# Trainium2, a fused attention and quantized-feed-forward layer: the first chunk's projections by seven products, and the squared norms' products behind a unit's scores

## The chip, the cores and the metric

The kernel runs on one core of a Trainium2 chip. The metric is the device time of one execution in microseconds. A profile of one further execution was taken; its rows are named by engine: PE is TensorE's products, PEld its weight loads, DVE is VectorE, ACT is ScalarE, POOL is GpSimd, SP is SyncE, which issues most loads and stores.

## The reference

For x of 8 x 1024 rows of 512 floats the reference computes (cut to what matters):

```python
x = x + layernorm(attention(layernorm(x), Wq, bq, Wk, bk, Wv, bv, Wo, bo))
x = x + layernorm(ffn(layernorm(x), weight))

# attention, 16 heads of 32
scores = einsum('bhid,bhjd->bhij', Q, K) / sqrt(32)
scores = where(causal_mask, -inf, scores) + where(causal_mask, 0, -(i - j))
out = einsum('bhij,bhjd->bhid', softmax(scores), V) @ Wo.T + bo

# ffn
xh = x @ hadamard(512)
xq = 4-bit rounding of xh, one scale a row
wq = ternary rounding of weight, one scale a row
return xq @ wq.T
```

## The kernel before, in words

The 8192 rows are 16 chunks of 512 rows (two chunks a sequence), and each chunk is four row tiles of 128. The penalty that grows with distance lets a query look at its own and the preceding keys of a band only, so a chunk needs its own keys and the last tile of the chunk before it. A chunk's work is cut into eight units: two halves of 256 queries by four groups of four heads. All of it is one program in an order written out by hand: every engine takes its instructions in the order in which the code names them, and semaphores tell it when an input is ready or a buffer free. No scheduler moves anything.

The steady loop (lines 819 to 916) runs over the chunks and, in each, over pairs of units. While chunk c's units are computed, the loop also does three other things: it projects chunk c+1 (class `Projections`), it normalises tiles of chunk c+2 (`norm_in`), and it runs the rest of the layer for finished row tiles (`rest`, two at a time). One pair of units is: scores of the first unit; values of the unit before; two of the products of the projection; parts of norm and rest; scores of the second unit; values of the first unit; more products. `scores` (line 559) writes the one PSUM tile `s` and ScalarE's Exp (line 585) reads it out with a bias; GpSimd masks (line 596) and adds the two key halves (line 610); `values` (line 616) multiplies with v (line 626) and with ones for the sums (line 637); VectorE divides (lines 655 to 660).

The projection of a chunk from the second on is made by seven products instead of eight, for each of q, k and v: the 512x512 product is cut into 2x2 blocks, sums of blocks of the weights and of xnT are made first, seven block products are computed in `ORDER` (line 379), and their sums are the result. `Weight.combine` and `Weight.replace` (lines 359 and 370) make the weights' sums once, on GpSimd; `replace` overwrites blocks of the weight. `Projections.combine` (line 387) makes the sums of xnT, `product` (line 405) issues four 128x256 products into one PSUM bank (line 417), and `drain` (line 422) adds the bank to the results: ScalarE for the first, VectorE for the others. Three PSUM banks (`Banks`, line 292) take turns for everything that is not scores or values; `bank(n)` names the one that the next tile takes.

The Exp's bias needs a bound on the scores. For the next chunk, `square` squares q and later k on ScalarE, `bound` (line 477) issues four small products that sum the squares by head (`norms_of`, line 333, 128x32 shapes in TensorE), `largest` reduces them on VectorE, and `multiply`, `spread_max` and `shift` (lines 490, 522 and 505) turn them into the bias. In each chunk of the loop, `bound` is called twice, in the pairs u = 4 (q) and u = 6 (k), ahead of the second unit's scores.

The first chunk cannot be projected under another chunk's units, so the start (lines 690 to 788) does it alone: the loads, the normalisation of four tiles and their transposes, then `project_v` four times, k four times and q four times (`project_qk`), each a 512x512 block column by four full 128x512 products (line 153) drained by ScalarE. Between them stand the norm tiles of chunk 1 (`ahead_norms`), the weights' sums on GpSimd and the steps of `prepare` (line 1170). `prepare` rounds the feed-forward weight to three values (a reduction for the scales, line 1175; thresholds, lines 1185 and 1187; transposes, line 1198), makes the row of scales (line 1213) and adds Wo times bv to the output bias: bv is spread over 128 columns and multiplied with Wo in four products (line 1221). Lastly `first.multiply` and `first.shift` make chunk 0's bias.

Of the kernel before, what the change touches and what calls it, by code (L numbers as in the profile page):

```python
# [40 lines left out]
def sandwich_kernel(  # L41
# [262 lines left out]
    def band():  # L304
# [71 lines left out]
        class Projections:  # L376
# [10 lines left out]
            def combine(self, which, engine=nc.gpsimd):  # L387

                x = self.ch.xnT
                b11, b12 = x[:, :HB, :HW], x[:, :HB, HW:]  # L390
                b21, b22 = x[:, HB:, :HW], x[:, HB:, HW:]
                if which == 0:
                    t = big.tile([P, KD, HB, HW], F32, tag="T", name=f"T_{self.ch.n}", bufs=1)
                    self.t = t
                    engine.tensor_tensor(t[:, 0], b12, b11, ALU.subtract)
                    engine.tensor_tensor(t[:, 1], b22, t[:, 0], ALU.subtract)
                    self.parts = {1: b11, 2: b21, 3: b22, 5: t[:, 0], 6: t[:, 1]}
                elif which == 1:
                    nc.gpsimd.tensor_tensor(self.t[:, 2], b22, b12, ALU.subtract)
                    self.parts[7] = self.t[:, 2]  # L400
                else:
                    nc.gpsimd.tensor_tensor(self.t[:, 3], self.t[:, 1], b21, ALU.subtract)
                    self.parts[4] = self.t[:, 3]
# [100 lines left out]

            def shift(self):


                ch = self.ch
                shift = small.tile([P, 1], F32, tag="shift", name=f"shift_{ch.n}")
                nc.gpsimd.tensor_tensor(shift, spread_max(self.diag, ch.n), half1, ALU.pow)  # L510
                nc.gpsimd.tensor_scalar(shift, shift, -SLACK, -0.5, ALU.mult, ALU.add)
                nc.gpsimd.tensor_scalar(shift, shift, ROUND, None, ALU.add)
                nc.gpsimd.tensor_scalar(shift, shift, ROUND, None, ALU.subtract)
                ch.bias = small.tile([P, 2, 2], F32, tag="bias", name=f"bias_{ch.n}")
                nc.gpsimd.tensor_scalar(ch.bias, decay_cols, shift, None, ALU.add)

# [158 lines left out]
        def start_rest(ch, t):  # L675
# [11 lines left out]
            )  # L687


        x0 = big.tile([P, TPC, D], F32, tag="pr", name="x0")  # L690
# [14 lines left out]
        ch.xnT = big.tile([P, KD, CT], F32, tag="xnT", name=f"xnT_{ch.n}")  # L705
        ch.kT = big.tile([P, KD, CT], F32, tag="kT", name=f"kT_{ch.n}")
        ch.qT = big.tile([P, KD, CT], F32, tag="qT", name=f"qT_{ch.n}")
        ch.v = big.tile([P, TPC, D], F32, tag="v", name=f"v_{ch.n}")
        made = []
# [17 lines left out]

        def squares_of_q(o0, o1):
            nc.scalar.activation(sqq[:, o0:o1, :], ch.qT[:, o0:o1, :], AF.Square)

# [7 lines left out]
        transposed(0)  # L738
        first = Projections(ch, None)
        prep = prepare(pools, wf_sb)  # L740
        ahead_steps = {0: "01", 1: "02", 2: "0", 3: "132", 4: "1", 5: "23", 6: "2", 7: "3", 8: "3"}
        for i in range(3 * KD):
            if i % 2 or not i:
                for t in ahead_steps.get(i, ""):
                    next(ahead_norms[int(t)])
            which, o = divmod(i, KD)
            if which == 0:
                project_v(pools, wv_sb, ch.v, ch.xnT, o, ch.n)
            elif which == 1:
                project_qk(pools, "k", wk_sb, bk_sb, ch.kT, ch.xnT, o, ch.n)  # L750
            else:
                project_qk(pools, "q", wq_sb, bq_sb, ch.qT, ch.xnT, o, ch.n)
            if i == 0:
                transposed(1)
                normalised(3)
                transposed(2)
            elif i == 1:
                transposed(3)
            elif i == KD - 1:
                prepare_q(wq_sb)  # L760
                nc.gpsimd.tensor_tensor(bqk_step[:, 0], bq_sb[:, HB:], bq_sb[:, :HB], ALU.subtract)
                nc.gpsimd.tensor_tensor(bqk_step[:, 1], bk_sb[:, HB:], bk_sb[:, :HB], ALU.subtract)
                weights[2].combine()
                weights[2].replace()
                weights[1].combine()
            elif i == 2 * KD - 1:
                weights[0].combine()
                weights[1].replace()
                sqk = squares(ch, "k", ch.kT)
                sqq = row.tile([P, KD, CT], BF16, tag="sq", name=f"sqq_{ch.n}", bufs=1)  # L770
            elif i == 2 * KD:
                ch.mk = largest_of(ch, "k", norms_of(ch, "k", sqk))
            elif i == 2 * KD + 2:
                squares_of_q(0, HB)
            if i and i % 2 == 0:
                for t in ahead_steps.get(i, ""):
                    next(ahead_norms[int(t)])
            if i in (KD, 6, 2 * KD):
                next(prep)
        squares_of_q(HB, KD)  # L780
        next(prep)
        next(prep)
        ch.mq = largest_of(ch, "q", norms_of(ch, "q", [sqq[:, o, :] for o in range(KD)]))
        first.multiply()
        next(prep)
        first.shift()
        next(prep)
        weights[0].replace(nc.vector)

# [20 lines left out]
        rests_due = ahead(start_rest(ch, t) for ch in chunks for t in range(TPC))  # L810
        def bank(at):
            pools.ps_m.named = at


# [4 lines left out]
        for at, ch in enumerate(chunks[:-1]):  # L819
# [7 lines left out]
            for u in range(0, 2 * NG, 2):  # L827

                new = Unit(ch, before, u)
                new.scores()  # L830
# [13 lines left out]
                proj.drain()  # L844
                norm = next(norms_due)
                steps(norm, 1)
                bank(two)
# [12 lines left out]
                steps(rest_b, 1)  # L860
                steps(rest_a, 1)
                if u >= 4:
                    bank(held)
                    proj.bound()

                new = Unit(ch, before, u + 1)
                new.scores()
                unit.values()
                if u >= 4:
                    held, one, two = one, two, held  # L870
                bank(held)
                proj.product()
                steps(rest_b, 1)
                if u >= 4:
# [295 lines left out]
    def prepare(pools, wf_sb):  # L1170
# [3 lines left out]
        ws = const.tile([P, KD], F32, name="wscale")  # L1174
        nc.vector.tensor_reduce(ws, w, AX.X, ALU.add, apply_absolute_value=True)
        nc.vector.tensor_scalar(ws, ws, 1.0 / D, SCALE_MIN, ALU.mult, ALU.max)
# [3 lines left out]
        nc.vector.tensor_scalar(lo, ws, -0.5, None, ALU.mult)  # L1180
        diag = row.tile([P, KD, P], F32, tag="u", name="wdiag", bufs=1)

        def ternary(k):
            below = row.tile([P, D], F32, tag="y", name=f"below_{k}", bufs=1)
            nc.vector.tensor_scalar(below, w[:, k, :], lo[:, k : k + 1], None, ALU.is_lt)
            tern = row.tile([P, D], BF16, tag=("qi", "qiT")[k % 2], name=f"tern_{k}", bufs=1)
            nc.vector.scalar_tensor_tensor(
                tern, w[:, k, :], hi[:, k : k + 1], below, ALU.is_gt, ALU.subtract
            )
            nc.vector.tensor_scalar(  # L1190
                diag[:, k, :], ident, ws[:, k : k + 1], 1.0 / QPOS, ALU.mult, ALU.mult
            )
            return tern

        def transposed(k, tern):
            pt = pools.ps_m.tile([P, KD, P], BF16, tag="pm", name=f"ternT_ps_{k}")
            for i in range(KD):
                nc.tensor.transpose(pt[:, i, :], tern[:, i * P : (i + 1) * P], ident_bf)
            nc.vector.tensor_copy(ternT[:, :, k * P : (k + 1) * P], pt)

        terns = [ternary(k) for k in range(2)]
        yield
        for k in range(2):
            transposed(k, terns[k])
        terns += [ternary(k) for k in range(2, KD)]
        yield
        nc.vector.tensor_copy(had0_sb, had_sb)
        nc.vector.memset(had0_sb[:, 0:1], 0.0)
        bvw = row.tile([P, KD, P], F32, tag="wT", name="bvw", bufs=1)
        nc.vector.tensor_copy(bvw, bvT_sb.unsqueeze(2).to_broadcast([P, KD, P]))  # L1210
        yield
        pr = pools.ps_m.tile([P, D], F32, tag="pm", name="wscale_ps")
        nc.tensor.matmul(pr, ones, diag.rearrange("p k q -> p (k q)"), start=True, stop=True)
        nc.vector.tensor_copy(wscale_row, pr)
        yield
        for k in range(2, KD):
            transposed(k, terns[k])
        yield
        ps = pools.ps_m.tile([P, D], F32, tag="pm", name="bo2_ps")
        for k in range(KD):  # L1220
            nc.tensor.matmul(
                ps, bvw[:, k, :], wo_sb[:, k, :], start=(k == 0), stop=(k == KD - 1)
            )
            if k == KD // 2 - 1:
                yield
        nc.vector.tensor_tensor(bo2, ps, bo2, ALU.add)
        yield
# [51 lines left out]
```

## Time and profile before

| | |
|---|---|
| median of 3 runs | 1396.66 us (1395.66 to 1398.48) |
| the profiled execution | 1396.07 us, its span 1394.3 us |
| granted TensorE clock | 0.995 of full speed |
| busy share of the span | PE 98%, PEld 69%, DVE 73%, ACT 49%, POOL 64% |
| span of the start, to the first scores | 61.94 us |

The span reaches from the first to the last instruction; the execution's own time is 1.8 us longer. In a line of the timeline the first figure is the start in us from the span's start and the second the duration; the number behind x is the count of records (an f32 product leaves two records), and a bracket names idle time just before and what ended it. In a line of the waits the figures are the sum in us, how many times, and the longest.

### The profile page before, as it was taken

The numbers are of one execution on the slowest core, as the hardware profiler recorded it, in microseconds if no ns is written. First come the engines' busy times: TensorE is split into PE (matmuls) and PEld (weight loads), VectorE is DVE, ScalarE is ACT, GpSimd is POOL, SyncE is SP. The second block draws the span as 40 slices with busy tenths as digits, with TensorE's granted clock in tenths as the row PEclk, the third lists the DMA queues.
The fourth block names the chain that finished last, engine by engine and source line by source line (L and its number), as shares of the span: only waits on it lengthen the run. The fifth ranks groups of instructions, "written<-read, shape, count | busy, mean of one in ns | idle before, by whom it ended". The sixth has DMA issues, their size and how long they took to land.

```text
span 1394.3 us, 35003 instructions
## 1 busy us (share of the span) xinstructions
PE 1363.4 (98%) x14504; PEld 967.5 (69%) x14504; DVE 1015.7 (73%) x2167; ACT 681.2 (49%) x1176; POOL 892.0 (64%) x1280
## 2 busy tenths in 40 slices
PE   9999999999999999999999999999999999999895
PEld 5577777777767777767776777777776777766553
DVE  5467777777777776777777777877777777777675
ACT  3345454545445455554545545445544545535442
POOL 4565758576576767658676676757757666665434
PEclk9999999999999999999999999999999999999998
DMA  6010011011011011011011011011101101000010
GB/s 228 8 47 24 24 47 46 24 47 47 24 47 47 24 47 47 32 39 47 30 41 46 25 47 47 28 43 47 40 31 47 47 24 47 25 23 32 32 39 33
DMA packets 31750, 58.23 MB, mean 42 GB/s; under 512 B 4064, under 2 KB 4448, under 8 KB 31584
## 3 DMA queue, kind: packets, MB, share of 16 engines
q1 hardware_dynamic: 30720, 54.87, 11.4%
q8 instruction: 116, 1.90, 0.5%
q10 hardware_dynamic: 864, 1.05, 0.2%
q14 instruction: 50, 0.41, 0.1%
HBM read 39.13 MB, written 16.78 MB: 40 GB/s over the span
## 4 chain that ended last, share of the span: by engine, by line


## 5 line engine op out<-in xcount | busy, mean ns | idle before, releaser
L585 ACT ACTIVATE pr<-s,bias 128x512 f32<-128x512 f32 (+1 forms) x512 | 295.3, 660 | 138.5 <-PE s L571 138.5
L610 POOL TENSOR_TENSOR both<-pr 128x1024 f32<-128x1024 f32 (+1 forms) x120 | 250.5, 2088 | 5.2
L153 PE MATMUL o_ps<-wo_sb,oT 128*128 128x512 f32 x512 | 236.1, 604 | 0.6
L596 POOL TENSOR_SCALAR_AFFINE_SELECT pr<-pr 128x1024 f32<-128x1024 f32 x128 | 150.0, 1172 | 108.2 <-ACT pr L585 103.8
L153 PEld LDWEIGHTS o_ps<-wo_sb,oT 128*128 128x128 f32 x512 | 93.2, 192 | 95.2 <-issue 92.5
L187 DVE TENSOR_TENSOR y<-o_ps,bo 128x512 f32<-128x512 f32 x64 | 44.2, 691 | 150.5 <-PE o_ps L153 150.5
L626 PE MATMUL av<-pr,v 128*32 128x128 f32 (+1 forms) x2816 | 130.7, 316 | 1.8 <-DVE oT L660 1.8
L571 PE MATMUL s<-qT,kT 32*64 32x192 f32 (+2 forms) x5632 | 119.9, 285 | 1.5 <-ACT pr L585 1.5
L571 PEld LDWEIGHTS s<-qT,kT 32*64 32x64 f32 x5632 | 99.8, 131 | 31.0 <-issue 21.6
L141 ACT ACTIVATE xn<-xc,nmr,rstd_n 128x512 f32<-128x512 f32 x60 | 48.8, 814 | 140.0 <-POOL nmr L139 140.0
L119 POOL TENSOR_SCALAR rstd_a<-mv_a 128x1 f32<-128x1 f32 x64 | 13.9, 217 | 142.7 <-DVE mv_a L127 141.5
L226 ACT ACTIVATE wT<-h_ps 128x512 f32<-128x512 f32 x64 | 38.2, 597 | 133.8 <-PE h_ps L218 133.8
L626 PEld LDWEIGHTS av<-pr,v 128*32 128x32 f32 x2816 | 74.9, 110 | 35.4 <-issue 1.8
L212 ACT COPY wT<-wT_ps 128x512 f32<-128x512 f32 x64 | 37.5, 585 | 123.4 <-PE wT_ps L210 123.4
L238 DVE TENSOR_REDUCE sc<-h_ps 128x1 f32<-128x512 f32 x64 | 44.1, 689 | 63.8 <-ACT wT L226 63.8
L119 POOL TENSOR_SCALAR rstd_c<-mv_c 128x1 f32<-128x1 f32 x64 | 14.7, 229 | 116.1 <-DVE mv_c L127 116.0
L285 POOL TENSOR_TENSOR y<-y,x 128x512 f32<-128x512 f32 x63 | 80.6, 1279 | 1.3 <-ACT y L284 1.3
L637 PE MATMUL av<-both,ones 128*32 128x256 f32 x960 | 74.2, 381 | 0.5 <-POOL both L614 0.5
L218 PEld LDWEIGHTS h_ps<-had_sb,wT 128*128 128x128 f32 x512 | 66.8, 192 | 6.2 <-ACT wT L212 3.3
L218 PE MATMUL h_ps<-had_sb,wT 128*128 128x128 f32 x512 | 68.1, 276 | 2.1 <-ACT wT L212 2.1
L153 PE MATMUL f_ps<-ternT,qiT 128*128 128x512 bf16 x256 | 66.2, 382 | 2.4 <-ACT qiT L257 2.4
L146 ACT COPY xnT<-xnT_ps 128x512 f32<-128x512 f32 x60 | 35.2, 586 | 56.8 <-PE xnT_ps L145 56.8
(213 smaller groups left out, 3100.7 us busy)
## 6 DMA issues: line engine op xcount, KB each, us to landing
xr<-in_x SPq DMA_DIRECT2D x64, 256.0 KB, 2.9
out<-y SPq DMA_DIRECT2D x63, 256.0 KB, 2.0
xc<-in_x SPq DMA_DIRECT2D x60, 256.0 KB, 2.7
wv_sb<-in_wvT ACTq DMA_DIRECT2D x4, 256.0 KB, 5.1
x<-in_x SPq DMA_DIRECT2D x4, 256.0 KB, 4.9
wk_sb<-in_wkT SPq DMA_DIRECT2D x1, 1024.0 KB, 6.7
wq_sb<-in_wqT SPq DMA_DIRECT2D x1, 1024.0 KB, 9.0
wf_sb<-in_wf SPq DMA_DIRECT2D x1, 1024.0 KB, 10.7
```

Of the source, the lines that this page charges most:

```text
L141: nc.scalar.activation(xn, xc, AF.Identity, bias=nmr, scale=r)
L153: nc.tensor.matmul(ps, lhs(k), rhs(k), start=(k == 0), stop=(k == KD - 1))
L187: nc.vector.tensor_tensor(y, ps, bo2, ALU.add)
L218: nc.tensor.matmul(xh[:, k * P : (k + 1) * P], wT[:, k, :], had_sb if k else had0_sb, start=True, stop=True,)
L238: nc.vector.tensor_reduce(sc, xh, AX.X, ALU.max, apply_absolute_value=True)
L285: nc.gpsimd.tensor_tensor(y2, y2, x1, ALU.add)
L571: nc.tensor.matmul(s[half * hp : (half + 1) * hp, hh, column[which] + c0 : column[which] + c1], kc.kT[hsl, g, k0 : k0 + hp], ch.qT[hsl, g, ...
L585: nc.scalar.activation(pr[:, :, r0:, own, cols], s5[:, :, r0:, own, cols], AF.Exp, bias=ch.bias[:, own, h : h + 1],)
L596: nc.gpsimd.affine_select(out=own, in_=own, compare_op=ALU.is_ge, fill=0.0, base=0, pattern=[[0, HPG], [0, 2], [1, P]], channel_multiplier=-1,
L610: engine.tensor_tensor(self.both[:, :, r0:], pr[:, :, r0:, 0, :], pr[:, :, r0:, 1, :], ALU.add)
L626: nc.tensor.matmul(av[hh * HD : (hh + 1) * HD, 0, qc : qc + w], kc.v[:, at, h * HD : (h + 1) * HD], pr[:, hh, sc : sc + w], start=(at_part ...
L637: nc.tensor.matmul(av[hh * HD : (hh + 1) * HD, 1, :], ones[:, :HD], self.both[:, hh].rearrange("p r c -> p (r c)") if own is None else sel ...
```

## The change

There are three parts. First, chunk 0's k and q are made by the seven products (`first.product` and `first.drain`, with `first.done` set to 7 for k and to 0 for q), and v stays as it was. For this the sums of wk stand on GpSimd during the projection of v, those of wq behind them, those of wv after q; the sums of chunk 0's xnT are made on VectorE; the steps of `prepare`, of the norm tiles and of the squares are spread anew between the products, with named banks at the end. The scales' reduction becomes four passes on ScalarE with a sum. Second, the bias is made of weighted rows: GpSimd multiplies the rows of Wo by bv and adds the four blocks, and one product with ones sums over the partitions. Third, in the steady loop `proj.bound()` is issued behind the second unit's scores instead of ahead of them. With these go smaller moves: the shift's last four operations of chunk 0 run on VectorE, the first norm tile of the loop starts ahead of the first scores, and for the first two pairs of chunk 0 the values of the first unit stand behind one product.

```diff
-    nc.gpsimd.tensor_tensor(self.t[:, 2], b22, b12, ALU.subtract)
+    engine.tensor_tensor(self.t[:, 2], b22, b12, ALU.subtract)
...
-            def shift(self):
+            def shift(self, engine=nc.gpsimd):
                 nc.gpsimd.tensor_tensor(shift, spread_max(self.diag, ch.n), half1, ALU.pow)
-                nc.gpsimd.tensor_scalar(shift, shift, -SLACK, -0.5, ALU.mult, ALU.add)
+                engine.tensor_scalar(shift, shift, -SLACK, -0.5, ALU.mult, ALU.add)
...
-        for i in range(3 * KD):
-            which, o = divmod(i, KD)
-            if which == 0:
-                project_v(pools, wv_sb, ch.v, ch.xnT, o, ch.n)
-            elif which == 1:
-                project_qk(pools, "k", wk_sb, bk_sb, ch.kT, ch.xnT, o, ch.n)
-            else:
-                project_qk(pools, "q", wq_sb, bq_sb, ch.qT, ch.xnT, o, ch.n)
...
+        for t in range(TPC):
+            if t == 0:
+                go(0, 1)
+            elif t == 1:
+                go(0, 2)
+            elif t == 3:
+                go(1, 3, 2)
+            project_v(pools, wv_sb, ch.v, ch.xnT, t, ch.n)
+            if t == 0:
+                transposed(1)
+                normalised(3)
+                transposed(2)
+                weights[1].combine()
+            elif t == 1:
+                transposed(3)
+                prepare_q(wq_sb)
+                weights[1].replace()
...
+            elif t == 2:
+                go(0)
+                for kind in range(3):
+                    first.combine(kind, nc.vector)
+            else:
+                weights[0].combine()
+                weights[0].replace()
+                next(prep)
+        kinds = len(Projections.ORDER)
+        first.done = kinds
+        for i in range(kinds):
+            first.product()
+            first.drain()
+            if i in (0, 2, 4):
+                go((1, 2, 3)[i // 2])
+            elif i in (1, 3):
+                go((2, 3)[i // 2])
+            next(prep)
+        sqk = squares(ch, "k", ch.kT)
+        first.done = 0
+        for i in range(kinds):
+            first.product()
+            first.drain()
+            if i == 1:
                 ch.mk = largest_of(ch, "k", norms_of(ch, "k", sqk))
...
+        weights[2].combine()
+        weights[2].replace()
...
         ch.mq = largest_of(ch, "q", norms_of(ch, "q", [sqq[:, o, :] for o in range(KD)]))
         first.multiply()
+        bank(0)
         next(prep)
-        first.shift()
+        bank(2)
+        go(3)
+        bank(1)
+        first.shift(nc.vector)
         next(prep)
...
+                if at == u == 0:
+                    norm = next(norms_due)
+                    steps(norm, 1)
                 new = Unit(ch, before, u)
                 new.scores()
...
-                if u >= 4:
-                    bank(held)
-                    proj.bound()
 
                 new = Unit(ch, before, u + 1)
                 new.scores()
-                unit.values()
+                if u >= 4:
+                    bank(held)
+                    proj.bound()
+                late = at == 0 and u < NG
+                if not late:
+                    unit.values()
...
                 proj.product()
+                if late:
+                    unit.values()
...
-        nc.vector.tensor_reduce(ws, w, AX.X, ALU.add, apply_absolute_value=True)
+        for k in range(KD):
+            nc.scalar.activation(below, w[:, k, :], AF.Abs, accum_out=ws[:, k : k + 1])
...
+        bvw = row.tile([P, D], F32, tag="wT", name="bvw", bufs=1)
+        nc.gpsimd.tensor_scalar(bvw, wo_sb[:, 0, :], bvT_sb[:, 0:1], None, ALU.mult)
+        for k in range(1, KD):
+            more = row.tile([P, D], F32, tag="w", name=f"bvw_{k}", bufs=1)
+            nc.gpsimd.tensor_scalar(more, wo_sb[:, k, :], bvT_sb[:, k : k + 1], None, ALU.mult)
+            nc.gpsimd.tensor_tensor(bvw, bvw, more, ALU.add)
...
-        for k in range(KD):
-            nc.tensor.matmul(
-                ps, bvw[:, k, :], wo_sb[:, k, :], start=(k == 0), stop=(k == KD - 1)
-            )
+        nc.tensor.matmul(ps, ones, bvw, start=True, stop=True)
         nc.vector.tensor_tensor(bo2, ps, bo2, ALU.add)
```

## The prediction

> **What bounds the kernel now.** I read the page first, then TensorE's waits, then the timelines of the start and of one stretch of the steady loop. The chain of waits answers with no piece here, so the bound is read from TensorE itself.
>
> ```profile
> PE 1363.4 (98%) x14504; PEld 967.5 (69%) x14504; DVE 1015.7 (73%) x2167; ACT 681.2 (49%) x1176; POOL 892.0 (64%) x1280
> ```
>
> Busy ends of PE are modelled, so 98% alone proves little. The waits of PE between 160 and 1290 us do: three, 0.6 us in all, in 1130 us.
>
> ```profile
> PE wT_ps L210 <- DVE u_v L453: 0.4, 2, 0.2
> PE wT_ps L210 <- DVE w L202: 0.2, 1, 0.2
> ```
>
> So PE's queue sets the end from the first projection to the tail, and a microsecond taken from it early shifts everything after. PE's timeline of the start (start, duration, engine, line, tiles, count, idle before) prices what is replaced:
>
> ```profile
> 24.87 3.60 PE L153 MATMUL k_ps<-xnT,wk_sb 128*128 128x512 f32 x8
> 28.31 0.60 PE L145 MATMUL xnT_ps<-ident,xn 128*128 128x128 f32 x4
> ...
> 55.73 1.02 PE L1213 MATMUL wscale_ps<-wdiag,ones 128*128 128x512 f32 x2
> 56.59 0.61 PE L1198 MATMUL ternT_ps<-ident_bf,tern 128*128 128x128 bf16 x8
> 57.54 0.61 PE L333 MATMUL nq<-sqq,head_rows 128*32 128x512 bf16 x4 [0.34 <-DVE wscale_row L1214]
> 58.08 1.98 PE L1221 MATMUL bo_ps<-wo_sb,bvw 128*128 128x512 f32 x4
> 59.90 0.38 PE L525 MATMUL m_ps<-diag,ones 128*128 128x128 f32 x2
> 60.12 1.88 PE L1221 MATMUL bo_ps<-wo_sb,bvw 128*128 128x512 f32 x4
> 61.94 0.77 PE L571 MATMUL s<-qT,kT 32*64 32x192 f32 x32
> ...
> 70.86 1.89 PE L417 MATMUL q_ps<-T,wq_sb 128*128 128x256 f32 x8
> 72.59 1.89 PE L417 MATMUL q_ps<-T,wq_s 128*128 128x256 f32 x8
> ```
>
> Start to start, a whole projection block of four products takes 3.44 us (24.87 to 28.31), one of the seven products 1.73 us (70.86 to 72.59), a single 128x512 product 0.86 us (55.73 to 56.59).
>
> **Start: what leaves PE.** Chunk 0's k and q are 8 blocks, 8 x 3.44 = 27.5 us; they become 14 products, 14 x 1.73 = 24.2, plus 0.1 for the one that follows the norms of k: minus 3.2. The output bias is four products (58.08 to 59.90 and 60.12 to 61.94), 3.64 us; it becomes one of 0.86: minus 2.8. Two waits of before lie in the replaced order: the norms of k take 0.85 us (44.09 to 44.94) and those of q 0.54 after 0.34 idle, against 0.33 in the steady loop: minus 1.0. The transposes of the norm tiles and of the ternary weights, and wscale, keep their number. Together minus 7.0.
>
> **Start: what is added, and which wait comes next.**
>
> ScalarE sums the absolute weights instead of VectorE's 2.25 us reduction: four 128x512 passes behind the last v copy (25.07 + 0.58). No row shows Abs; the nearest are the Square with a sum at 0.60 and the Identity from SBUF at 0.82, so 2.2 to 3.3 us, and I take 0.60 + 0.15 for the chained sums, to 28.6. The drain of k's first product (two Identities, 0.85) queues behind them, to 29.5. Three PSUM banks rotate, so the third product, ready at 24.87 + 1.73 + 0.44 + 1.73 = 28.8, waits 0.7.
>
> VectorE's scale operations wait for those sums, and k's second drain stands behind them on VectorE. GpSimd then combines wq: its queue waits for the tile that lands at 24.2 us, so its sums run from about 26.5. What that costs VectorE is on the timeline of both:
>
> ```profile
> 27.18 1.27 POOL L365 TENSOR_TENSOR wv_s<-wv_sb 128x512 f32<-128x512 f32 x1
> 27.35 1.13 DVE L1176 TENSOR_SCALAR wscale<-wscale 128x4 f32<-128x4 f32 x1
> 28.53 1.28 POOL L366 TENSOR_TENSOR wv_s<-wv_s,wv_sb 128x512 f32<-128x512 f32 x1
> 28.59 1.25 DVE L1180 TENSOR_SCALAR wscale_lo<-wscale 128x4 f32<-128x4 f32 x1
> ```
>
> Four elements a partition take 1.13 and 1.25 us, because each ends when GpSimd's two-tensor operation ends (28.45, 29.81); alone the same form took 0.17. With two such waits k's second drain ends between 32 and 33, the fourth product was ready at about 31.7: I take 1.0 (0 if nothing collides, 2.6 if every operation does).
>
> VectorE in the rest of k's loop: eight drain operations (6 x 0.69, 2 x 0.47), the threshold operations (4 x 0.47, 4 x 0.75, 4 x 0.28), 3 x 0.17, statistics 0.87 and two copies 0.74 make 13.2 us from 28.6. PE offers 13.1 us there up to q's second product. Nearly even, so some bank waits: 0.4 (0 to 3).
>
> Chunk 0's sums of xnT (four at 0.69) stand on VectorE before the late tile; VectorE idled 12.0 us there, so they cost nothing. wk's sums run on GpSimd from 13.7 us, in its idle 11.6, wanted at 28.8: nothing. The weighted rows are four tensor-scalar (about 1.5) and three additions (1.27) on GpSimd, 9.8 us, wanted only after q: nothing. wv's five operations (7.3 us in before) now stand behind them, ahead of the shift's power: they end about 1 us before it is due, and beyond that the first Exp is late one for one.
>
> k's squares (0.69 + 1.99) lie under q's first two products (3.46); q's first drain queues behind them: 0.2.
>
> Before, VectorE's chain from q's norms to the diagonal (58.19 to 59.40) lay under the bias product of 1.82. Now only transposes (about 0.9) cover some 1.4 us: 0.5.
>
> The shift's last four operations, 0.19 to 0.31 each on GpSimd, move to VectorE at about 0.21: even. But the next norm tile's steps now stand ahead of the first mask on GpSimd: 0.22 + 0.57 + 0.27 plus waiting for statistics that queue behind the shift. The first values are delayed, though one product is put ahead of them: 0.4 (0 to 1.5). The loads that move with these steps stand on SP with nothing urgent behind.
>
> Waits: 0.7 + 1.0 + 0.4 + 0.2 + 0.5 + 0.4 = 3.2. Start: 3.2 - 7.0 = minus 3.8, between minus 6.5 and minus 0.5.
>
> **Steady loop.** In 15 chunks, two squared-norm groups each, 30 in all, move from before the second unit's scores to behind them. PE's weight loads and products around one:
>
> ```profile
> 516.48 0.10 PEld L333 LDWEIGHTS <-head_rows 128*32 128x32 bf16 x4 [0.42 <-issue]
> 516.80 0.85 PEld L571 LDWEIGHTS s<-qT,kT 32*64 32x64 f32 x48 [0.23 <-issue]
> 517.73 0.81 PEld L626 LDWEIGHTS av<-pr,v 128*32 128x32 f32 x24
> 518.51 0.24 PEld L637 LDWEIGHTS av<-both,ones 128*32 128x32 f32 x8
> 518.62 0.62 PE L637 MATMUL av<-both,ones 128*32 128x256 f32 x8
> ```
>
> Norms, scores and values have shapes 128x32, 32x64, 128x32. Where the shape changes, the first load starts with the first product (516.48; 516.80 against 516.81; 517.73): it hides behind nothing. Where it stays 128x32, from values to sums, the loads start at 518.51, 0.11 ahead of their product, under the products still running. Today a norm group costs 0.33 (516.48 to 516.81). Behind the scores it is followed by values of its own shape, whose load (0.110) can then run under it: minus 0.11 a group, 30 x 0.11 = 3.3. Bounds: nothing, or more if the scores, 0.33 earlier, also move GpSimd out of VectorE's way. Seven of the 15 k-groups are followed, two products later, by a lag of VectorE before wT's transposes (at 290.90 a product takes 2.14 to the transposes instead of 1.73), which may swallow it: I take 22 x 0.11 = 2.4. Exp of the unit before ends 6.7 us ahead, so the earlier scores wait for nothing; the maximum on VectorE begins at 517.92, after its own queue, and the norms behind the scores would end at about 517.8: nothing.
>
> On this the Trainium skill, "TensorE: Matmul & The Clock Gate", Part 3, says the contrary: weight loads overlap running products only where the row group differs. Norms and values both span all rows, so by that rule the steady term would be nothing and the sum 1392.9. The loads at 518.51, of all 128 rows under products of all rows, do not agree with it.
>
> **Sum.** 3.8 + 2.4 = 6.2. The profiled execution took 1396.07 (span 1394.3), 0.6 below the median 1396.66: it would take 1389.9, and the median 1390.5.
>
> **Rivals.**
>
> Weight loads stay exposed behind the norms, so the steady term is zero: 1396.66 - 3.8 = 1392.9. For it, a bf16 group ahead of an f32 one in this shape is shown nowhere; against it, the rows at 518.51. Chance 0.20. The rule of the Trainium skill's page on TensorE would give this result.
>
> Nothing collides: waits of the start shrink by about 2.0, all 30 groups save: 1396.66 - 5.8 - 3.3 = 1387.6. For it, most of VectorE's threshold operations fall where GpSimd waits for the last norm tile. 0.13.
>
> The start eats itself: bank waits of about 6 instead of 3.2 and half of the steady term: 1396.66 - 1.0 - 1.2 = 1394.5. 0.10.
>
> Slower: VectorE becomes the bound of k's loop, held by GpSimd at every operation that both need the same access for. Seven operations of before between 27.35 and 38.94 took 8.94 us against 2.59 alone, 0.91 more each. If all 15 were held, 13.6 us come on top of an even balance, 12.2 more than the 1.4 already counted: 1390.5 + 12.2 = 1402.7. It decides from 6.2 us, seven more held operations. Against it: inside GpSimd's tensor-scalar of 32.65 to 34.52 VectorE's 0.47 and 0.75 went at full speed, and about five two-tensor operations are left to collide with. 0.07.
>
> **How the numbers follow.** A measurement of this kernel tells about 0.2% from no change, 2.8 us: faster is below 1393.9, slower above 1399.5. The forecast holds 0.50. Faster: 0.50 + 0.13 + 0.16 of the first rival's 0.20 = 0.79. Same: 0.04 + 0.09 = 0.13. Slower: 0.07 + 0.01 = 0.08. The range goes from below the second rival, 1386.8, to the third, 1394.5; the slower case and half of the third are left out.
>
> **What would show it.** Right: the first scores at 57 to 59.5 us instead of 61.94; bank waits of PE at the third and fourth product of k; norm groups that take about 0.22 from their start to that of values, with value loads starting ahead of them; the distance from one chunk's norms to the next's shorter by some 0.2 us. Wrong: first scores after 61; norms still at 0.33 behind the scores; waits of PE for the mask or for VectorE in every chunk that are not there now.

## The result and the profile after

The changed kernel takes 1388.70 us, median of five runs (1388.63 to 1390.49), against 1396.66 us for the kernel before (1394.46 to 1398.48): a ratio of 0.9944, 95% interval 0.9932 to 0.9955, 8.0 us less by the medians. Run once more beside later experiments it took 1388.18 against 1394.42: 0.9954 (0.9940 to 0.9967), or 6.2 us less. The forecast was 6.2 us less.

The profiled execution took 1388.64, its span is 1386.9, 7.35 us below the span before (both taken to the last hundredth from the trace). Part 1 of the page after, and the waits of PE between 160 and 1290 us (us in total, times, longest):

```profile
PE 1350.5 (97%) x14483; PEld 972.7 (70%) x14546; DVE 1021.3 (74%) x2187; ACT 681.6 (49%) x1181; POOL 905.4 (65%) x1285
```

```profile
PE wT_ps L210 <- DVE u_v L453: 1.5, 7, 0.6
PE wT_ps L210 <- DVE w L202: 1.5, 7, 0.2
```

PE is busy 12.9 us less and the span only 7.35 shorter, but the two busy times can't be compared as they stand: the bf16 products f_ps have 256 records in the profile before and 193 in this one (193 also in e5 below, the same kernel as before), 3.6 us of busy time, and 1.7 us of the time before are a stretch at half clock, shown below. The waits ahead of wT's transposes, three before, are fourteen now, and these have to be taken apart. Those for u_v stand in the last unit of every second chunk, where the transposes follow their product after 2.06 us before and 2.05 now: there nothing has changed, the idle time has only passed the 0.15 us from which the view shows it. (One of the seven, of 0.6, belongs to the tail, which reaches into this window now.) Those for w are new: in the second unit of the same chunks the transposes follow after 2.11 us instead of 1.81. Something has begun to hold PE there. The start on PE's timeline (start, duration, tiles, count, idle before and its releaser):

```profile
29.74 1.96 PE L417 MATMUL k_ps<-T,wk_s 128*128 128x256 f32 x8 [0.45 <-issue]
...
31.97 1.89 PE L417 MATMUL k_ps<-T,wk_sb 128*128 128x256 f32 x8
...
38.16 1.97 PE L417 MATMUL k_ps<-xnT,wk_s 128*128 128x256 f32 x8 [0.34 <-DVE u_k L466]
...
53.63 1.02 PE L1274 MATMUL bo_ps<-bvw,ones 128*128 128x512 f32 x2
...
56.64 0.46 PE L525 MATMUL m_ps<-diag,ones 128*128 128x128 f32 x2 [0.55 <-DVE diag L519]
57.03 0.77 PE L571 MATMUL s<-qT,kT 32*64 32x192 f32 x32
```

The first scores come at 57.03 instead of 61.94. The bias product is one of 1.02. The third product of k, its seventh and m_ps wait; the fourth, in this execution, does not.

Around a norm group, weight loads on PE's load timeline, and the norms and values on PE's:

```profile
511.48 0.85 PEld L571 LDWEIGHTS s<-qT,kT 32*64 32x64 f32 x48 [0.42 <-issue]
512.40 0.10 PEld L333 LDWEIGHTS <-head_rows 128*32 128x32 bf16 x4
512.41 0.98 PEld L626 LDWEIGHTS av<-pr,v 128*32 128x32 f32 x24
513.39 0.23 PEld L637 LDWEIGHTS av<-both,ones 128*32 128x32 f32 x8
...
512.40 0.40 PE L333 MATMUL nq<-sqq,head_rows 128*32 128x512 bf16 x4
512.63 1.04 PE L626 MATMUL av<-pr,v 128*32 128x256 f32 x24
```

The loads of the values start at 512.41, 0.01 us after those of the norms: they no longer wait until the norms' products are through. From the norms' start to that of the values it takes 0.226 us; before, from the norms to the scores, 0.330 (means of 30 groups).

The whole by stretches, from the starts of the 128 score groups (L571), eight to a chunk:

| stretch | before | after | difference |
|---|---|---|---|
| up to k's first product | 24.87 | 25.23 | +0.36 |
| to the first scores | 37.06 | 31.79 | -5.27 |
| chunk 0's units (to the 9th scores) | 69.71 | 70.15 | +0.44 |
| loop (9th to 121st) | 1164.33 | 1162.82 | -1.51 |
| 121st to 125th | 28.57 | 26.89 | -1.68 |
| rest | 69.75 | 70.06 | +0.31 |

In this pair of profiles the start gave more than forecast, the loop less; how far single profiles differ is shown below. The row of 1.68 us is no work of the change: in a second profile of the kernel before (run e5 below) it is 26.88. The view by windows (us, busy time of PE, PEld, DVE, ACT, POOL, then the granted clock, DMA share, GB/s) shows the half clock in the first profile, and none in e5, in which the same products come 1.7 us later:

```profile
1302.00:1306.00 4.00, 4.00 (x7) 1.57 (x6) 0.00 (x0) 1.83 (x4) 0.00 (x0) 0.60 0.04 14
```

```profile
1302.00:1306.00 4.00, 3.52 (x54) 1.96 (x36) 0.89 (x2) 3.10 (x6) 0.72 (x1) 1.00 0.41 131
```

For 3.4 us around 1302 the granted clock was half, and eight 128x512 products took 5.35 us instead of 3.65 in e5. Ahead of the last 13 us, two of the fourteen profiles have such a stretch in the tail (before and e4), e6 has two elsewhere, the others none, so in the pair it belongs to an execution and not to the change. The Trainium skill, "TensorE: Matmul & The Clock Gate", Part 1, describes a free-running activity window of about 3.4 us after which an idle array falls to half clock: the length agrees. But the page asks for a whole idle window, and PE had idled only 1.49 us and then 0.47 in the 3.4 us before; in e5 it idled the same 1.49 us and kept full clock. That the window's phase decides, no run here shows.

### The profile page after: what moved, and what is told of

Same layout as the page of the kernel before. It is cut to its first block, busy times and chain, and to the rows that moved or that the text cites. A ratio compares the mean times of both kernels' runs of the same rounds, so it can differ in the third digit from the quotient of the medians.

```text
span 1386.9 us, 35067 instructions
## 1 busy us (share of the span) xinstructions
PE 1350.5 (97%) x14483; PEld 972.7 (70%) x14546; DVE 1021.3 (74%) x2187; ACT 681.6 (49%) x1181; POOL 905.4 (65%) x1285
## 4 chain that ended last, share of the span: by engine, by line
## 5 line engine op out<-in xcount | busy, mean ns | idle before, releaser
L571 PEld LDWEIGHTS s<-qT,kT 32*64 32x64 f32 x5632 | 99.7, 130 | 36.7 <-issue 26.8
L571 PE MATMUL s<-qT,kT 32*64 32x192 f32 (+2 forms) x5632 | 119.8, 284 | 1.5 <-ACT pr L585 1.5
L153 PE MATMUL f_ps<-ternT,qiT 128*128 128x512 bf16 x193 | 62.6, 382 | 5.9 <-ACT qiT L257 2.6
```

What stands on the lines that cost most here:

```text
L153: nc.tensor.matmul(ps, lhs(k), rhs(k), start=(k == 0), stop=(k == KD - 1))
L571: nc.tensor.matmul(s[half * hp : (half + 1) * hp, hh, column[which] + c0 : column[which] + c1], kc.kT[hsl, g, k0 : k0 + hp], ch.qT[hsl, g, ...
```

## The experiments

The kernel before took 1394.4 to 1396.0 us beside them.

**The two halves apart.** e1 is the kernel before with the norms behind the scores, e2 the changed kernel with them back ahead:

```diff
+                new = Unit(ch, before, u + 1)
+                new.scores()
                 if u >= 4:
                     bank(held)
                     proj.bound()
-                new = Unit(ch, before, u + 1)
-                new.scores()
```

> The kernel before with the third part alone: the squared norms' products behind the second unit's scores. Theory (one change of shape less, taken back at the chunk's turn): each norm group takes 0.226 us to the values instead of 0.33 to the scores and the values' own group 0.02 less, 0.26 us a chunk; but GpSimd is busy without a gap at u = 0, so PE waits some 0.15 us more before wT's transposes there, and a chunk gains only 0.1 us: 1.5 us over the loop, 1395.2 against 1396.7, the first scores unmoved at 62 us. Rival (the wait at u = 0 has to do with the new start): the whole 30 x 0.13 = 3.9 us is gained, 1392.8.

> The changed kernel with the norms' products put back ahead of the scores: the start alone. Theory: first scores at 57.0 to 57.5 us as in the changed kernel, 4.4 us won after the first units and the distance of two chunks back at 166.45 us: 1390.2 if the half-clock stretch near 1302 us is absent as in the changed kernel's profile, 1392.0 if it is there. Rival (start and loop depend on each other): less than 3 us or more than 6 us won before the first full chunk.

e1: 1392.58, ratio 0.9982 (0.9973 to 0.9991), loop 1162.91. e2: 1390.89, ratio 0.9972 (0.9961 to 0.9982), loop 1165.02, first scores 33.33 after k's first product. The halves add up: 2.4 and 4.1 us. What the norms are worth in the loop depends on which profiles are compared: 1.4 us from before to e1, as e1's theory had it, 2.2 from e2 to after and from e5 to e10 (a second profile of each kernel, below), 2.9 from e2 to e10. The changed kernel's loop alone differs by 0.7 between after and e10. The forecast for the 28 groups of these chunks is 2.2, and 28 times the 0.104 by which each group shrank would be 2.9. So the size of the loss isn't settled by single loops; where it lies is, by the distances inside the chunks.

**Where the loop's gain went.** Distances from one score group to the next, means of six even and six odd chunks:

| kernel | 2nd to 3rd, even | odd | 3rd to 4th, odd | 5th to next chunk's 1st, even | odd |
|---|---|---|---|---|---|
| before | 9.66 | 10.27 | 10.73 | 43.24 | 42.86 |
| after | 9.96 | 10.29 | 10.74 | 42.97 | 42.62 |
| e10: after, once more | 9.92 | 10.26 | 10.73 | 42.96 | 42.62 |
| e11: before, third sum on VectorE | 9.53 | 9.50 | 10.58 | 43.21 | 42.85 |
| e3: after, third sum on VectorE | 9.55 | 9.50 | 10.58 | 42.97 | 42.62 |
| e7: after, third and fourth on VectorE | 9.07 | 9.50 | 10.58 | 42.96 | 42.62 |

The second half of a chunk, where the norms lie, gains 0.25. Then the stretch from the second to the third scores of the next even chunk takes 0.30 longer (0.26 in e10), so about half of what two chunks gain is given back there. That stretch has no norms in it. In it the rest of the layer runs for one row tile: GpSimd's root of the statistics (rstd_a), VectorE's x1 and its sums u and w, and wT's transposes on PE, each waiting for the one before. GpSimd, VectorE and PE there, in the changed kernel:

```profile
387.51 1.29 POOL L399 TENSOR_TENSOR T<-xnT 128x512 f32<-128x512 f32 x1
388.89 0.22 POOL L119 TENSOR_SCALAR rstd_a<-mv_a 128x1 f32<-128x1 f32 x1
```

```profile
389.80 0.75 DVE L194 SCALAR_TENSOR_TENSOR x<-y,rstd_a,xr 128x512 f32<-128x512 f32 x1 [0.76 <-POOL rstd_a L120]
```

```profile
391.70 1.89 PE L417 MATMUL q_ps<-T,wq_sb 128*128 128x256 f32 x8
393.81 0.79 PE L210 MATMUL wT_ps<-ident,w 128*128 128x128 f32 x4 [0.22 <-DVE w L202]
```

The statistics mv_a are ready at 388.39, but the third sum of T (L399) holds GpSimd until 388.80, and it started so late because GpSimd's queue has no gap over 0.1 us from 374.29 on, where the key sums of the unit before begin. Behind it come the root and all that waits for it. In the kernel before the same sum ran, the queue was as full, and the place in PE's timeline reads so:

```profile
396.71 1.89 PE L417 MATMUL q_ps<-T,wq_sb 128*128 128x256 f32 x8
398.52 0.79 PE L210 MATMUL wT_ps<-ident,w 128*128 128x128 f32 x4
```

No wait is shown, yet there are two. A product's row is 1.89 long and the next may start 1.73 after it, here 1.81 after; and the four transposes last 0.79 instead of 0.60, as the last of them waits inside the group. With the key sums started 3.12 us ahead of the chunk's first scores the root (rstd_a) ended 12.32 after them; after the change, which brings the scores forward but not GpSimd, it is 2.86 and 12.61.

e3 moves the third sum:

```diff
-                    proj.combine(1)
+                    proj.combine(1, nc.vector)
```

> The changed kernel with the third sum of xnT (L399 there), which stands on GpSimd ahead of the attention statistics' root at u = 0, moved to VectorE, which idles 3 us there. Theory (GpSimd's queue at the chunk's turn takes back the loop's gain): the root is ready 0.5 us earlier, PE's wait before wT's transposes at u = 0 goes, 0.11 to 0.3 us a chunk: 1.5 to 4 us, 1384.7 to 1387.2. Rival (that wait has another cause, VectorE's own sums): nothing changes, 1388.7, or VectorE's 0.69 us a chunk makes it slower.

1380.33 us, ratio 0.9894 (0.9879 to 0.9909), loop 1153.98: 8.84 us less than after (8.1 less than e10), where at most 4 was expected. GpSimd now waits for the statistics instead of the reverse:

```profile
387.83 0.23 POOL L119 TENSOR_SCALAR rstd_a<-mv_a 128x1 f32<-128x1 f32 x1 [0.61 <-DVE mv_a L127]
```

Was the hold there before the change? The first attempt, e5, made the same edit in the kernel before, whose method names GpSimd at the sum itself, so that nothing was moved: the run repeats the kernel before (1395.15 against 1394.42, ratio 1.0002, 0.9993 to 1.0011). Its expectation therefore went untested until e11, which edits the sum:

```diff
-                    nc.gpsimd.tensor_tensor(self.t[:, 2], b22, b12, ALU.subtract)
+                    nc.vector.tensor_tensor(self.t[:, 2], b22, b12, ALU.subtract)
```

> Kernel before, with the third sum of each chunk's transposed norms (T, L399 of after) on VectorE instead of GpSimd; start and norms untouched. If GpSimd's queue already held the second half of each chunk's first pair of units before the change, the distance from the second to the third scores falls from 9.66 and 10.27 us (chunks in turn) to about 9.55 and 9.50, the next one from 10.73 to 10.58: 1.03 us in two chunks, some 7.5 us in all, so about 1387.5 against 1395 for the kernel before. If that lag comes only with the earlier scores of the change, under 1.5 us: 1393.5 or more. By the first, the loop stays 3.6 us longer than with the same move in the changed kernel (1153.98), which is then the worth of the norms alone.

> Kernel before, with the third sum of T issued on VectorE in every chunk of the loop, start and norms as before. If GpSimd's queue already held the stretch from a chunk's second scores to its third before the change, that distance falls from 9.66 and 10.27 us (even and odd chunks) to about 9.55 and 9.50, the next one in odd chunks from 10.73 to 10.58: 1.03 us in two chunks, loop from 9th to 121st scores about 1157 instead of 1164.3, time about 1387.5 against 1394.5. The loop then stays 3.6 us longer than with the same move in the changed kernel (1153.98), which is what the norms alone are worth once GpSimd holds nothing. If the lag comes only with the earlier scores of the change: loop 1162.8 or more, time above 1393.

1389.17 us, ratio 0.9952 (0.9938 to 0.9965), loop 1157.05 where 1157 was expected: GpSimd held the kernel before too, for the 7.3 us of its loop that this move brings. And with this sum out of GpSimd's way in both, the norms are worth 1157.05 - 1153.98 = 3.07 us in the loop, 0.110 for each of its 28 groups (0.130 against e9 below, whose loop has e3's code and took 1153.41).

e6 leaves the third sum on GpSimd and moves the first two:

```diff
-                    proj.combine(0, nc.gpsimd if at else nc.vector)
+                    proj.combine(0, nc.vector)
```

> Changed kernel, with the first two sums of T (1.28 and 1.33 us on GpSimd) on VectorE in every chunk, the third left on GpSimd. If what counts is the length of GpSimd's queue without a gap from the end of one chunk to the root for the rest's statistics, it gains as much as moving the third sum: loop from 9th to 121st scores 1154 to 1156 instead of 1162.8, in all about 1380 to 1382. If what counts is only that the third sum stands between those statistics and their root, the loop stays at 1162.8 and the time at about 1387. If VectorE with 1.7 us more ahead of the drains becomes late, waits of PE for VectorE at the first products of a chunk, and slower than 1388.

1420.10 us, ratio 1.0188 (1.0175 to 1.0202), its runs spread from 1412 to 1424 with granted clocks from 0.995 down to 0.987. The profile is that of the fastest run, loop 1185.89. Both the first and the last reading came true in different stretches. From the second to the third scores the distances are 9.57 and 9.50, as with the third sum moved, so it is the length of the queue that counts and not that one operation. But from the first to the second they grew by 1.84 and 2.52: on VectorE the two sums (1.18 and 1.52) stand ahead of the rest's rounding, and PE waits for it, fourteen times in the loop.

```profile
306.30 0.40 PE L255 MATMUL qiT_ps<-ident_bf,qi 128*128 128x128 bf16 x4 [2.06 <-DVE qi L248]
```

e7 moves the third and the fourth sum:

```diff
-                    proj.combine(1)
+                    proj.combine(1, nc.vector)
...
-                    proj.combine(2)
+                    proj.combine(2, nc.vector)
```

> Changed kernel with the third and the fourth sum of T on VectorE, the first two on GpSimd. The fourth stands on VectorE ahead of the rest's x1, in 1.04 us of idle time there, and no longer holds the first adds of w on VectorE (1.2 to 1.5 us instead of 0.42 each in the profile with the third sum moved). If those adds end last ahead of w's transposes: the 0.38 us of wait left there goes, loop some 3 to 5 us below 1153.98, time 1375 to 1378. If the mask's select, which stays on GpSimd, holds them anyway: within 1 us of the run with the third sum alone (1380.3). If the fourth sum is held by GpSimd's root for the rest's statistics and pushes x1 back: up to 1385.

1377.94 us, ratio 0.9872 (0.9856 to 0.9887), loop 1149.72. By the first of its readings: the sums of w on VectorE, which took 1.21 and 1.49 us beside GpSimd's fourth sum in e3, take 0.43 and 0.42. The even chunk's stretch falls to 9.07, and the place reads:

```profile
389.56 1.89 PE L417 MATMUL q_ps<-T,wq_sb 128*128 128x256 f32 x8
391.29 0.60 PE L210 MATMUL wT_ps<-ident,w 128*128 128x128 f32 x4
```

1.73 to the transposes, 0.60 for them. Against this floor the kernel before lost 0.59 + 0.77 + 0.15 = 1.5 us in two chunks, by estimate some 11 us in all (e11 shows 7.3 of it), of which the view of waits named 0.6. One wait is in every kernel here, this one too: the 2.05 us ahead of the transposes in the last unit of every second chunk; the last units of the other chunks take 1.73. Its cause was not looked for.

**The start.** e10 is the changed kernel unaltered, e8 the changed kernel with the Abs sums one projection earlier and the bias product ahead of the scales' row:

```diff
             elif t == 2:
                 go(0)
                 for kind in range(3):
                     first.combine(kind, nc.vector)
+                next(prep)
             else:
                 weights[0].combine()
                 weights[0].replace()
-                next(prep)
...
-        nc.vector.tensor_copy(wscale_row, pr)
+        nc.scalar.copy(wscale_row, pr)
```

> The changed kernel once more, unaltered, on the same chip as these runs. By the reading that the start differs between executions with the landing of the late norm tile: first scores 31.8 to 33.3 us after k's first product, the fourth product of k waiting 0 to 1.1 us; loop from 9th to 121st scores 1162.8 to within 0.3; time 1386.5 to 1388.5, a stretch of 3.4 us at half clock in the tail present or not (1.7 us).

> Changed kernel, start only: the four Abs sums of the weights go to ScalarE one projection earlier, ahead of the last v copy (from about 23 us instead of 25.9), and the bias product stands ahead of the scales' row, whose copy goes to ScalarE. By the prediction's terms the third product of k no longer waits (0.45 in the profile of after), the fourth waits 0 to 0.5 instead of 0 to 1.1, and the column maximum's product 0.25 instead of 0.55: first scores 30.7 to 31.3 us after k's first product instead of 31.8 to 33.3; loop unchanged at 1162.8; time 0.8 to 2 us below the changed kernel. Rival: VectorE as a whole sets the pace of k's loop, and the waits only move on to later products: 31.8 to 33.3 as before, no gain.

e10: first scores 33.15 us after k's first product; the loop, 1162.12, is further from 1162.8 than the 0.3 allowed for. Fourth product on PE, and two of VectorE's operations ahead of its bank's drain:

```profile
32.81 1.97 PE L417 MATMUL k_ps<-T,wk_sb 128*128 128x256 f32 x8 [1.14 <-DVE kT L447]
```

```profile
29.33 1.24 DVE L1215 TENSOR_SCALAR wscale_lo<-wscale 128x4 f32<-128x4 f32 x1
30.61 1.45 DVE L1222 TENSOR_SCALAR below<-wf_sb,wscale_lo 128x512 f32<-128x512 f32 x1
```

The first ends with GpSimd's two-tensor sum of wq (29.27 to 30.55), the second outlasts the next one (30.51 to 31.77). In the profile of after that is shown above GpSimd was some 1.8 us ahead, because the late norm tile's statistics began at 22.55 instead of 24.37, and the same two took 0.16 and 0.49. Other profiles with this start (e2, e3, e4) show 0.90 to 1.12 of wait there, e6 0.41 and e7 0.47. That the tile's landing is what differs is read from the rows; no run changed it alone.

The kernel before varies at its start as well, and more: its first scores come 37.06 us after k's first product in before, 36.68 in e1, 38.45 in e11 and 38.96 in e5, where PE waits twice for the squares of k:

```profile
45.40 0.39 PE L333 MATMUL nk<-sqk,head_rows 128*32 128x512 bf16 x2 [1.40 <-ACT sqk L346]
46.34 0.39 PE L333 MATMUL nk<-sqk,head_rows 128*32 128x512 bf16 x2 [0.55 <-ACT sqk L346]
```

In e11 these waits are 0.89 and 0.55; in before and e1 none is shown. With the changed start six profiles lie between 31.79 and 33.33. The means, 37.8 and 32.7, are 5.1 us apart, and single pairs give anything from 3.4 to 7.2.

e8: 1386.87, ratio 0.9941 (0.9927 to 0.9954), first scores 31.52 after k's first product. Third and fourth product no longer wait, but 0.43 us returns at the seventh (0.77 instead of 0.34), so the rival was right in part:

```profile
30.92 1.89 PE L417 MATMUL k_ps<-T,wk_sb 128*128 128x256 f32 x8
...
37.78 1.97 PE L417 MATMUL k_ps<-xnT,wk_s 128*128 128x256 f32 x8 [0.77 <-DVE u_k L466]
```

e4 puts the bias back to four products, without the weighted rows on GpSimd:

```diff
-        nc.tensor.matmul(ps, ones, bvw, start=True, stop=True)
+        for k in range(KD):
+            nc.tensor.matmul(
+                ps, bvw[:, k, :], wo_sb[:, k, :], start=(k == 0), stop=(k == KD - 1)
+            )
```

> The changed kernel with the output bias made as before, by four products of a spread bv, in the same place; the weighted rows are gone from GpSimd. Theory (PE's time decides): three products of 0.86 us more, 2.6 us slower, 1391.3, first scores at 59.6. Rival (the weighted rows hold VectorE in k's loop and delay wv's sums): the four products come for less than 1.5 us, because the threshold operations of 1.58 and 1.06 us fall back to 0.5 and 0.75.

1393.05, ratio 0.9987 (0.9978 to 0.9996); first scores 37.30 after k's first product, 4.17 later than in e3, which waits as long at the fourth product. The products are 2.6 of it (56.35 to 59.88 against 0.95 us). The rest, 1.6, is a cost that nobody had named: without the weighted rows, wv's two-tensor sums come onto GpSimd at 38.5 instead of 48.4 and hold VectorE's threshold operations (0.98, 1.15 and 1.28 us against 0.48, 0.74 and 0.63), and q's loop waits three times. In e4's profile 1.7 us is the half-clock stretch.

**The best version.** e9 joins e8's start to e3, e12 joins it to e7.

> Changed kernel with the third sum on VectorE and the start with the Abs sums one projection earlier, the bias product ahead of the scales' row. The two lie in different stretches, so their gains add: first scores 31.5 us after k's first product, loop 1154.0, time 1378.5 to 1379.5 (1.0 to 1.6 below the third sum alone on the same chip). If the start's gain is only a matter of when the late norm tile lands: 1380 as without it.

> The changed kernel with what gained in the other runs put together: third and fourth sum of T on VectorE, Abs sums one projection earlier, bias product ahead of the scales' row. If the pieces add: first scores 31.5 us after k's first product, loop 1149.7, time about 1.0 us below the two sums alone: 1376 to 1377. If the start's gain disappears again in chunk 0, where the first distances already moved: 1378.

e9: 1378.58, ratio 0.9880 (0.9864 to 0.9895). e12: 1375.98, ratio 0.9862 (0.9845 to 0.9878), loop 1149.73, first scores 31.52: the pieces add, and this is the fastest kernel here, some 12 us below the change (1388.18 and 1388.70).

## Why the prediction was right, point by point

- **Work leaving the start, minus 7.0, and the waits that take its place.** Right in kind and nearly in size. Start to start the third product waited 0.61 (0.7 forecast; its row names issue in one profile and POOL in the other, but in both its bank's drain on ScalarE ends 0.1 us ahead of it), the rest of k's loop 0.34 idle at the seventh (0.4), q's first drain 0.22 (0.2), the diagonal 0.55 idle and 0.77 start to start (0.5), chunk 0 took 0.44 longer in spite of its two norm groups (0.4). The fourth product's 1.0 is the one that varied: 0 in the first profile, 0.41 to 1.14 in the others. Without it the forecast to the first scores is minus 5.2, and the first pair has minus 5.27; with it minus 4.2, and the means of all profiles give minus 5.1. That the first pair agrees to a tenth is luck: the term of 1.0 for waits of before was read from one profile, and the wait for k's squares in it, 0.5 us of that term, is nothing in e1 and some 2.4 in e5.
- **Norms behind the scores, 0.11 a group.** Right, cost and mechanism: 0.104 directly, 0.110 by e11 against e3 (0.130 against e9).
- **22 of 30 groups count, minus 2.4.** (30 less the seven named are 23, a tenth of a microsecond more.) The size can't be told from right: 2.2 was forecast for the loop and 1.4 to 2.9 measured. The mechanism was wrong. The lag of VectorE that was to swallow a quarter, at 290.90 in the last unit of every second chunk, stayed as it was, 2.06 us and 2.05, and the second half of these chunks gained its 0.27 in full. What took gain back is another place, the stretch from the second to the third scores of even chunks, which grew by 0.30 (0.26 in e10). Its cause was GpSimd's queue, which the prediction did not name.
- **"PE's queue sets the end."** Only in part. GpSimd set one stretch of every chunk, for 7.3 us of the kernel before by e11 and about 11 by estimate, and the reason given for the opposite, 0.6 us of waits, was an effect of how PE's rows are drawn. One of the signs that were to show the prediction wrong did come: waits of PE for VectorE that were not there before, for w, in every second chunk. And the distance between the norms of one chunk and of the next fell by 0.1 us (166.48 to 166.29 for two chunks), not by 0.2.
- **The rivals.** Exposed loads: refuted by the loads at 512.41. By the rule of the Trainium skill, "TensorE: Matmul & The Clock Gate", Part 3, that the prediction cites, the norms would still take 0.33, and the measurement, 0.226, does not agree; the same Part also lets a load go ahead into a background weight buffer, which would fit, and no run here shows whether it is that. What agrees is the Trainium skill's "TensorEngine Tiling (Array Packing)", Key Properties, which says that changing the tiling mode drains the array: where 32x64 scores give way to 128x32 norms the load starts only with its product, at 512.40, and the load at 512.41 does not wait so. Nothing collides: the first profile's start looked so, its repetitions did not. The start eats itself, and VectorE as bound of k's loop: refuted by first scores at 57 to 58.
- **Outside the prediction.** Of the first pair's 7.35 us, 1.68 are the half-clock stretch of the execution before. Without it that pair gives 5.7; the second comparison gives 6.2 and the medians of the first 8.0. With starts of before that lie 2.3 us apart, and with loops of one kernel 0.7 apart, 6.2 to the tenth is luck; that the time falls by 6 to 8 us is not.

## What to carry to other kernels

Take the distance from one group's start to the next and compare it with the shortest such distance of the same pair of groups: that shows waits of which the idle column shows a part or nothing. Before work is made shorter on the engine that looks like the bound, look for a stretch in each period in which another engine's queue has no gap; part of what is gained ahead of that stretch is given back in it, here about half. A sum that can run on two engines belongs where the queue has idle time at that very place, and the same move one step earlier (e6) cost 23 us in the loop, where this one (e3) brought 8 to 9. And profile the kernel before more than once: what one execution shows as a wait to be saved may be none in the next.

## What the runs showed of the hardware

- Loads of 128x32 bf16 norms and 128x32 f32 values follow each other 0.01 us apart and hide under products, from one type to the other (512.40 and 512.41); after 32x64 scores the first load starts with its product (512.40).
- The sum taken with a ScalarE pass is a row of its own: 0.63 us for the 128x512 Abs, and 0.18 to 0.20 for reading the accumulator.
- A VectorE operation on four elements took 0.16 to 1.25 us, by what GpSimd ran beside it. Against GpSimd's two-tensor sums it ended with them (30.57 and 30.55 in e10).
- Half clock for 3.4 us in the tail of some executions, 1.7 us of time, after PE had idled 1.49 us; in e6 twice in the loop, after 2.05.
